# A scan kernel's order of work: a fourth product buffer, new due times, an ordered operand, and one more chunk before the loop's end

## The chip, the cores and the metric

The kernel runs on one core of one Trainium2 chip. A core has five engines that run side by side and meet only at semaphores: TensorE (PE in the profile; PEld is its weight load), VectorE (DVE), ScalarE (ACT), GpSimd (POOL) and SyncE (SP, which here only issues transfers). The metric is the device time of one execution, in microseconds: 31468.83 us is the median of three runs before the change (31461.65 to 31485.9). A profiled execution also gives a time for every instruction.

## The reference, cut to what matters

The input is a batch of 8 images of 128 channels and 64 x 64 points. A deformable 3 x 3 convolution is added to it. Its result is read as 8 sequences of 4096 tokens, and a selective scan runs over them; a mixture of experts follows.

```python
x = x + _L0_conv_ref(_gn(x), ...)              # deformable 3x3, four corners per tap
t = _to_tokens(x)                              # 8 x 4096 tokens of 128
xs, z = jnp.split(_ln_t(t) @ W_in, 2, axis=-1)
delta, Bv, Cv = xs @ W_delta, xs @ W_B, xs @ W_C
deltaA = jnp.exp(jnp.einsum('bld,dn->bldn', delta, A))
def step(state, inp):                          # state: 8 x 256 x 256
    dA_i, dB_i, x_i, C_i = inp
    state = dA_i * state + dB_i * x_i[:, None, :]
    return state, jnp.einsum('bdn,bn->bd', state, C_i)
t = t + (y * silu(z)) @ W_out                  # y: the steps' outputs
t = t + top-2 mixture of 8 experts of _ln_t(t)
```

The scan's state has 8 x 256 x 256 numbers, and each of the 4096 steps multiplies all of them by a decay, adds an outer product, and contracts them with a vector.

## The kernel before, in words

After a preparation (`prepare`, `images`: group norm, offsets, a table of cells in DRAM), a loop of 8 iterations covers 512 steps each. 16 steps are a block (`BL`), 2 steps a chunk (`CH`). On chip the state's 256 indices lie on 128 partitions in two halves, so that 8 images x 2 halves make 16 units of 256 columns. `SETS` deals them into five groups: groups 0 and 1 of four units and group 2 of three units live in SBUF (`ht`), group 3 of four units and group 4 of one unit live in PSUM (`ud`, `us`).

One step does this:

- `pair`: each group's state is multiplied by its decay `et` into a product buffer, by GpSimd for groups 0 to 2 and by VectorE for groups 3 and 4 (line 1310). Groups 0 and 1 share the pool `mt`, of three four-unit buffers; group 2 uses `m3`, group 3 `md`, group 4 `mh`, of two each.
- `units`: TensorE makes the outer products in three lots, into the single PSUM tile `up` for the groups in SBUF, and added in place onto `ud` and `us` for the others. VectorE adds product and `up` into `ht` (line 1325); ScalarE copies the products of groups 3 and 4 back to PSUM (line 1330), before the lot that adds to them.
- `contract`: TensorE contracts the products with `zc` into `yp`, groups 0 and 3 first, then 1, 2 and 4. A product buffer returns to its pool when its sum or copy and its contraction are both done.

For a later chunk, `decays` makes the exponents on TensorE in 19 groups, through three PSUM banks, and `grow` takes their exponentials on ScalarE into one of two `et` buffers (line 1224); it waits for all products of the chunk two before, which used the same buffer. `load_rows`, `load_terms` and `copy_c` bring the chunk's operands (`rt`, `uu`, `zc`), the first two through transfers on SP's queue.

Beside it, once a block: `conv_load` and `conv_gather` (nine indirect transfers that GpSimd issues in its own queue, line 724, into `g` buffers), `conv_scale` (VectorE, three taps at a time: 12 operations, after which three `g` buffers come free, into `w` buffers), `conv_mix` (transposes, the convolution's sum, a norm), `project` (the projections; its first matmuls after `xst` compute the rows, with a strided view of `xst` as one operand), `stores`, and `behind` (the gate, the output projection, the routing, the experts, the store).

The order on every engine is written out by a planner, `Schedule.run`, when the program is built. Each of these generators is a thread that yields operations with a modelled duration and a due time, in steps. The planner keeps a modelled clock for each engine, takes the engine that could start earliest, and among its operations that could start within a short wait (`"wait"` of `DUE`) picks the one due first. The chip then runs this order as it stands: every engine's queue is in order, and a late operation holds up all that is queued behind it. Windows such as `project` spread their due times evenly over a span of steps. At the loop's end the planner starts afresh, from the state that `before` lists: what is ready at the seam.

Of the kernel before, what the change touches and what calls it, by code (L numbers as in the profile page):

```python
# [15 lines left out]
P = 128  # L16
# [9 lines left out]
NH = 2  # L26
# [25 lines left out]
QP = 3  # L52
REC = 5 * TAPS
# [13 lines left out]
def dve_ns(n, scaled=0):  # L67
# [4 lines left out]
    "gather": -0.04,  # L72
    "add": 0.23,
    "state": -0.33,
    "back": 1.16,
    "exp": (0.77, 1.65),
    "decay": (-0.1, 1.61),
    "unit": 0.33,
    "contract": 1.65,
    "project": (6.72, 11.35),  # L80
    "behind": (0.16, 13.12),
    "conv_mix": (1.0, 18.4),
    "conv_scale": (-0.99, 14.0),
    "same": 0.1,
    "wait": (200, 100, 100, 50),
# [8 lines left out]
class Due:  # L94


    def __init__(self, at, gap=0.0):
        self.at, self.gap = at, gap


class Op:


    def __init__(self, eng, ns, fn, lat=None, mode=FULL, need=None, free=(),
                 sets=(), chain=True, then=None, lock=None, due=None):
# [5 lines left out]
        self.chain, self.then, self.lock, self.due = chain, then, lock, due  # L111


class Thread:
    def __init__(self, gen):
        self.gen, self.t, self.cur = gen, 0.0, None
        self.due, self.gap = 0.0, 0.0


class Schedule:  # L120


    def __init__(self, pools, events=()):
# [5 lines left out]
        self.threads = []  # L129

# [5 lines left out]
    def step(self, th, value):  # L136
        try:
            th.cur = th.gen.send(value)
            while isinstance(th.cur, Due):
                th.due, th.gap = th.cur.at, th.cur.gap  # L140
                th.cur = th.gen.send(None)
# [7 lines left out]
    def run(self):  # L149
        while self.threads:  # L150
# [12 lines left out]
            ready = []  # L163
            for th in self.threads:
# [4 lines left out]
                if o.need is not None:  # L169
                    if not self.pools[o.need]:  # L170
                        continue
                    at = max(at, min(x[0] for x in self.pools[o.need]))
# [6 lines left out]
                ready.append((at, due, th))  # L179
# [25 lines left out]
            if o.due is None:  # L205
                th.due += th.gap
# [15 lines left out]
def kernel(  # L222
# [344 lines left out]
    mt = several(3, [P, 4 * DIN], FP, "mt")  # L567
    m3 = several(2, [P, 3 * DIN], FP, "m3")
    md = several(2, [P, 4 * DIN], FP, "md")
    mh = several(2, [P, DIN], FP, "mh")  # L570
# [12 lines left out]
    gt4 = several(5, [P, 4 * P], FP, "g")  # L583
    wt = several(6, [P, P], FP, "w")
# [4 lines left out]
    xst = fix.tile([P, 2, P], FP, name="xst")  # L589
    dpt = fix.tile([P, 3, DIN], BF, name="dpt")  # L590
# [3 lines left out]
    yt = fix.tile([P, DIN], FP, name="yt")  # L594
# [6 lines left out]
    se = fix.tile([P, P], FP, name="se")  # L601
    ot = fix.tile([P, P], FP, name="ot")
    nst = {w: fix.tile([P, 12], FP, name=f"n{w}") for w in "tm"}

    ud = psf.tile([P, 4 * DIN], FP, name="ud")
    up = psf.tile([P, 4 * DIN], FP, name="up")
    yp2 = psf.tile([P, 2, DIN], FP, name="yp")
    yp, us = yp2[:, 0, :], yp2[:, 1, :]
    state = ht + [ud, us]
    banks = [psf.tile([P, 512], FP, name=f"bank{k}") for k in range(3)]  # L610
# [898 lines left out]
```

## Time and profile before

| | us |
|---|---|
| median of 3 runs | 31468.83 |
| lowest and highest | 31461.65, 31485.9 |
| profiled execution | 31237.92 |
| its span, first to last instruction | 31236.1 |
| first product of the scan starts | 589.9 |
| last product of the scan ends | 31203.7 |

The profiled execution's mean granted TensorE clock is 0.975 of full speed. The page's first part gives each engine's busy time and its share of the span. The groups that follow give a line, an engine, the tiles written and read, the count, the busy time, the mean duration in ns, and the idle time of the engine just ahead of them with the instruction that ended it. A list of waits sums that idle time by who ended it: in total, how often, and the longest. A wait for several semaphores is put down to the one that came last.

### The profile page before, as it was taken

What the parts mean: (1) busy time and instruction counts of PE and PEld (TensorE: products, weight loads), DVE (VectorE), ACT (ScalarE), POOL (GpSimd) and SP (SyncE); (2) the same over time, 40 slices, a digit from 0 to 9 for tenths busy, and PEclk for the clock granted to TensorE, in tenths of its full rate; (3) what the DMA queues carried; (4) which work ended last, traced back from release to release, by engine and by line L of the source; (5) the groups of instructions that cost most, each with busy time, mean ns of one, the idle gap of its engine ahead of it and who ended that gap; (6) DMA issues with size and microseconds to landing.
All of it is one profiled execution on the core that took longest, in us unless ns stands there. A gap on an engine that the chain in (4) does not pass through costs nothing. (4 is left out here: it accounts for less than half of the span.)

```text
span 31236.1 us, 831602 instructions
## 1 busy us (share of the span) xinstructions
PE 28259.1 (90%) x303717; PEld 15288.6 (49%) x303717; DVE 26324.7 (84%) x47747; ACT 25431.0 (81%) x57825; POOL 28812.6 (92%) x14692
## 2 busy tenths in 40 slices
PE   6999989999899998999989999899998999989998
PEld 2544444544444444445444444444444444444544
DVE  5888888888888888888888888888888888888888
ACT  3888888888888887888888888888887888888888
POOL 3999999999999999999999999999999999999999
PEclk8999999999999999999999999999999999999999
DMA  5222222222222222222222222222222222222222
GB/s 128 60 57 60 58 57 57 60 58 59 56 60 58 59 60 56 59 58 60 57 58 57 60 57 60 55 61 59 58 60 56 58 58 60 57 58 58 60 57 56
DMA packets 4782745, 1873.06 MB, mean 60 GB/s; under 512 B 3445427, under 2 KB 4616504, under 8 KB 4777592
## 3 DMA queue, kind: packets, MB, share of 16 engines
q1 hardware_dynamic: 4578768, 1167.03, 18.8%
q0 software_dynamic: 191904, 625.53, 7.3%
q8 instruction: 2417, 39.60, 0.5%
q10 hardware_dynamic: 7944, 26.87, 0.3%
q14 instruction: 1712, 14.02, 0.2%
HBM read 1284.96 MB, written 532.52 MB: 58 GB/s over the span
## 5 line engine op out<-in xcount | busy, mean ns | idle before, releaser
L1224 ACT ACTIVATE et<-bank 128x448 f32<-128x448 f32 (+1 forms) x40980 | 19045.6, 527 | 3626.9 <-PE bank L687 3020.5
L1310 POOL TENSOR_TENSOR mt<-et,ht 128x1024 f32<-128x1024 f32 x8192 | 19282.7, 2370 | 1470.3 <-PE yp L687 873.7
L687 PE MATMUL bank<-rt,alhs 126*128 126x224 bf16 (+1 forms) x81960 | 12273.7, 254 | 1446.2 <-ACT et L1224 646.8
L1325 DVE TENSOR_TENSOR ht<-mt,up 128x1024 f32<-128x1024 f32 x8192 | 9967.2, 1217 | 2659.9 <-PE ud L687 1858.5
L687 PEld LDWEIGHTS <-alhs 126*128 126x128 bf16 x81960 | 6764.4, 98 | 7662.1 <-issue 6817.5
L687 PE MATMUL yp<-mt,zc 128*32 128x256 f32 x65536 | 8719.8, 388 | 152.1 <-POOL mt L1310 75.8
L1310 POOL TENSOR_TENSOR m<-et,ht 128x768 f32<-128x768 f32 x4096 | 7480.4, 1826 | 38.9 <-DVE ht L1325 11.3
L687 PE MATMUL up<-uu 32*128 32x256 bf16 x45056 | 4838.3, 275 | 598.6 <-DVE ht L1325 523.5
L1310 DVE TENSOR_TENSOR md<-et,ud 128x1024 f32<-128x1024 f32 x4096 | 4973.2, 1214 | 110.7 <-PEq L1442 43.3
L687 PE MATMUL yp<-m,zc 128*32 128x256 f32 x24576 | 4451.6, 391 | 156.1 <-POOL m L1310 147.9
L1325 DVE TENSOR_TENSOR ht<-m,up 128x768 f32<-128x768 f32 x4096 | 3892.5, 950 | 566.1 <-PE up L687 527.7
L687 PE MATMUL yp<-md,zc 128*32 128x256 f32 x32768 | 4359.7, 387 | 0.0
L1330 ACT COPY ud<-md 128x1024 f32<-128x1024 f32 x4096 | 4275.0, 1044 | 93.7 <-DVE md L1310 84.7
L687 PEld LDWEIGHTS yp<-mt,zc 128*32 128x32 f32 x65536 | 3273.9, 110 | 1622.0 <-issue 544.9
L687 PEld LDWEIGHTS <-uu 32*128 32x128 bf16 x65541 | 1613.7, 92 | 3121.3 <-issue 2882.9
L724 POOL DMA_INDIRECT g<-table,rec x2322 | 2265.1, 975 | 411.1 <-issue 244.3
L687 PE MATMUL yp<-mh,zc 128*32 128x256 f32 x8192 | 2483.8, 385 | 0.0
L1310 DVE TENSOR_TENSOR mh<-et,yp 128x256 f32<-128x256 f32 x4096 | 1704.6, 416 | 452.1 <-PE yp L687 429.2
L687 PEld LDWEIGHTS yp<-m,zc 128*32 128x32 f32 x24576 | 1587.8, 109 | 926.2 <-issue 422.9
L1330 ACT COPY yp<-mh 128x256 f32<-128x256 f32 x4096 | 1595.4, 389 | 355.8 <-PE yp L687 218.3
L757 DVE SCALAR_TENSOR_TENSOR bank<-g,rec,bank 128x128 f32<-128x128 f32 x4644 | 1640.7, 353 | 84.6
L687 PE MATMUL ud<-uu 32*128 32x256 bf16 x16388 | 1623.8, 276 | 0.1
(207 smaller groups left out, 22566.9 us busy)
## 6 DMA issues: line engine op xcount, KB each, us to landing
rt<-rz SPq DMA_DIRECT2D x14350, 22.5 KB
uu<-pr SPq DMA_DIRECT2D x8196, 36.0 KB
pr<-dpt SPq DMA_DIRECT2D x3084, 48.0 KB
pr<-bpt SPq DMA_DIRECT2D x3084, 48.0 KB
rz<-dst SPq DMA_DIRECT2D x6939, 21.0 KB
g<-table,rec POOLq DMA_INDIRECT x2322, 3.5
rec<-recs SPq DMA_DIRECT2D x2064, 2.8 KB
table<-xc SPq DMA_DIRECT2D x24, 858.0 KB
```

Source lines behind the costliest of these rows:

```text
L687: nc.tensor.matmul(out, lhs, rhs, start=start, stop=stop, **kw)
L724: nc.gpsimd.indirect_dma_start(out=g, out_offset=None, in_=table, in_offset=bass.IndirectOffsetOnAxis(ap=rec[b % 2].bitcast(I32)[:, j : j ...
L757: nc.vector.scalar_tensor_tensor(out, gq, s, acc, ALU.mult, ALU.add)
L1224: nc.scalar.activation(ec[:, :, :, P * f + d0 : P * f + d0 + n], ps[:, m * f * NH : m * (f + 1) * NH].rearrange("p (h d t) -> p h t d", h= ...
L1310: (nc.gpsimd if g < QP else nc.vector).tensor_tensor(like(g, m), part(g, c, lo), like(g, state[g]), ALU.mult)
L1325: lambda m=m: nc.vector.tensor_tensor(ht[g], m, up[:, :n], ALU.add),
L1330: ACT, act_ns(n, True), lambda m=m: nc.scalar.copy(state[g], m),
```

## The change

- `mt` gets a fourth buffer. To make room, `g` goes from five to four, `w` from six to five, `yt` becomes the same tile as `yy`, `se` the same as `tn2`, and `ot` the same as `tn2t`.
- Lots, contractions, state tiles and sums become general (`LOTS`, `CLOTS`, `PIECES`); with the values given, each step has the same instructions of the same size. The order of the matmuls within the second contraction and the second lot changes.
- The due times change: windows get inner points between which they run straight; each group has its own time for its sum, copy and lots; a product's turn goes by its width (0, 4/11, 8/11 of a step in place of thirds). The second contraction is due half a step earlier. The modelled cost of a product becomes 167 + 2.105 n ns in place of 25 + 2.237 n, and of a gather 1150 in place of 970.
- Windowed work due more than 14.37 steps after the latest product or gather planned is passed over as long as other work is ready.
- The rows' operand is copied by ScalarE into a second tile, `xsl`, in the order in which the matmuls read it.
- At the seam, and before the loop, two chunks instead of one have their decays taken and their operands loaded.

```diff
-    mt = several(3, [P, 4 * DIN], FP, "mt")
+MBUF = {"mt": (4, 4), "m3": (2, 3), "md": (2, 4), "mh": (2, 1)}
...
-    gt4 = several(5, [P, 4 * P], FP, "g")
-    wt = several(6, [P, P], FP, "w")
+    gt4 = several(NGB, [P, 4 * P], FP, "g")
+    wt = several(5, [P, P], FP, "w")
...
-    yt = fix.tile([P, DIN], FP, name="yt")
+    yt = yy
...
-    se = fix.tile([P, P], FP, name="se")
-    ot = fix.tile([P, P], FP, name="ot")
+    se, ot = tn2, tn2t
...
-    "gather": -0.04,
-    "add": 0.23,
-    "state": -0.33,
-    "back": 1.16,
-    "exp": (0.77, 1.65),
-    "decay": (-0.1, 1.61),
-    "unit": 0.33,
-    "contract": 1.65,
-    "project": (6.72, 11.35),
-    "behind": (0.16, 13.12),
-    "conv_mix": (1.0, 18.4),
-    "conv_scale": (-0.99, 14.0),
-    "same": 0.1,
-    "wait": (200, 100, 100, 50),
+    "gather": -4.86,
+    "add": (0.57, -0.4, 0.79),
+    "state": (-0.42, -0.27),
+    "back": (1.56, 1.06),
+    "exp": (0.77, 1.68, 0.51),
+    "decay": (-0.13, 1.19, 0.537),
+    "unit": (0.31, -0.0, 0.07),
+    "contract": (1.63, 1.14),
+    "project": (6.72, 11.35, 0.448, 0.486, 0.75),
+    "behind": (0.05, 13.12, 0.25, 0.521, 0.685),
+    "conv_mix": (1.0, 18.37, 0.318, 0.497, 0.75),
+    "conv_scale": (-0.99, 14.1, 0.293, 0.5, 0.759),
+    "same": 0,
+    "wait": (200, 100, 100, 0),
+    "lead": 14.37,
...
-                ready.append((at, due, th))
+                ahead = o.due is None and due > self.now + DUE["lead"]
+                (later if ahead else ready).append((at, due, th))
+            ready = ready or later
...
             yield Op(
                 ACT, act_ns(DIN),
                 lambda: nc.scalar.copy(xst, wk[:, :DIN].rearrange("p (a b) -> p a b", a=2)),
-                free=release(wk),
+            )
+            yield Op(
+                ACT, act_ns(DIN),
+                lambda: nc.scalar.copy(
+                    xsl, wk[:, :DIN].rearrange("p (a b l) -> p a l b", a=2, b=QI)
+                ), free=release(wk),
             )
...
-                    xlb[:, h], start=(h == 0), stop=(h == 1),
+                    xsl[:, h].rearrange("p l b -> p (l b)"), start=(h == 0), stop=(h == 1),
...
-            s.add(decays(range(1, NC + 1)))
-            s.add(grow(range(1, NC + 1)))
-            s.add(load_rows(range(2, NC + 2)))
-            s.add(load_terms(range(1, NC + 1)))
-            s.add(copy_c(range(1, NC + 1)))
+            s.add(decays(range(2, NC + 2)))
+            s.add(grow(range(2, NC + 2)))
+            s.add(load_rows(range(3, NC + 3)))
+            s.add(load_terms(range(2, NC + 2)))
+            s.add(copy_c(range(2, NC + 2)))
```

## The prediction

> **What bounds the kernel now.** First the page's busy shares, then GpSimd's groups with the idle time ahead of them, then the list of its waits.
>
> ```profile
> span 31236.1 us, 831602 instructions
> PE 28259.1 (90%) x303717; PEld 15288.6 (49%) x303717; DVE 26324.7 (84%) x47747; ACT 25431.0 (81%) x57825; POOL 28812.6 (92%) x14692
> ...
> L1310 POOL TENSOR_TENSOR mt<-et,ht 128x1024 f32<-128x1024 f32 x8192 | 19282.7, 2370 | 1470.3 <-PE yp L687 873.7
> L724 POOL DMA_INDIRECT g<-table,rec x2322 | 2265.1, 975 | 411.1 <-issue 244.3
> ```
>
> ```profile
> POOL mt L1310 <- PE yp L687: 873.7, 518, 4.2
> POOL mt L1310 <- DVE ht L1325: 231.8, 364, 2.2
> POOL mt L1310 <- POOLq L1442: 185.9, 7, 26.9
> POOL mt L1310 <- ACT et L1224: 146.0, 343, 26.0
> POOL g L724 <- DVE w L757: 71.6, 268, 9.0
> ```
>
> GpSimd carries the run, TensorE is close behind. From the starts of GpSimd's products: a step without gather or wait lasts 6.43 us, a gather adds 1.13, so a block of 16 steps with its 9 gathers could take 16 x 6.43 + 9 x 1.13 = 113.1 us. Over 240 blocks away from the seams it takes 118.7. Counting the idle time by the step's place in the block, the wait on "PE yp" sits at two places only: 1.1 us at step 8, and 2.4 us at step 11. There a product has no free mt buffer, because the third product back has not been contracted. The next view cuts two blocks into steps 8-9, 10-14 and 15-23.
>
> ```profile
> 13335.70:13350.24 14.54, 13.22 (x160) 6.92 (x161) 13.27 (x23) 12.08 (x27) 12.97 (x7) 1.00 0.31 42
> 13350.24:13388.86 38.62, 37.56 (x396) 21.28 (x396) 32.83 (x56) 32.90 (x75) 36.40 (x20) 1.00 0.38 76
> 13388.86:13453.72 64.86, 57.52 (x628) 30.22 (x626) 55.31 (x108) 54.06 (x124) 63.05 (x33) 0.97 0.20 53
> ```
>
> ```profile
> 13570.83:13585.38 14.55, 13.23 (x160) 6.92 (x161) 13.29 (x23) 12.08 (x27) 12.97 (x7) 1.00 0.28 41
> 13585.38:13626.84 41.46, 40.43 (x396) 23.50 (x396) 32.79 (x56) 32.93 (x75) 36.35 (x19) 0.92 0.35 71
> ```
>
> The columns are length, then PE, PEld, DVE, ACT and POOL busy, then the granted clock. In steps 10-14 TensorE is full (37.56 of 38.62 us), in steps 15-23 it has 7.3 us to spare. The second block differs by its clock, and its stretch is 2.84 us longer. Here are its GpSimd rows, steps 10 and 11:
>
> ```profile
> 13587.71 2.37 POOL L1310 TENSOR_TENSOR mt<-et,ht 128x1024 f32<-128x1024 f32 x1
> 13590.03 1.82 POOL L1310 TENSOR_TENSOR m<-et,ht 128x768 f32<-128x768 f32 x1
> 13595.97 4.71 POOL L1310 TENSOR_TENSOR mt<-et,ht 128x1024 f32<-128x1024 f32 x2 [4.12 <-PE yp L687]
> ```
>
> The wait is 4.12 us where the undisturbed block has 1.24. The granted clock is 0.50 from 13587.3 for 6.8 us. In all, 669 us of half clock fall into step 10, 6.83 us at a time: 98 dips. Blocks with one last 119.9 us, blocks without any 117.0. The sum below holds nothing for dips beyond what sits inside the mt wait. TensorE's longest gap just ahead of this dip is 0.68 us. [...]
>
> **The change, part by part.** *A fourth mt buffer.* The product at step 11 then needs the fourth product back, whose contraction ended at 13347.3 in the first block, 9.4 us before GpSimd was ready for it (13356.7). Bounds: nothing, or all 873.7 us (3.4 a block). What is late next is TensorE. Without moving its work, steps 10-14 can shrink from 38.62 to its 37.56 us, and steps 8-9 from 14.54 to its 13.22: 2.4 us. A dip's lag can now run into the slack of steps 15-23. I take 2.5 us a block, the TensorE bound being the nearest row: 256 x 2.5 = 640 us gained. [...]
>
> *Rows' operand copied in order.* One more ACT copy a block (L903's mean 377 ns; 257 of them, 97 us of ACT), ahead of the exponentials in ACT's queue; the first row matmul waits for it. The matmuls lose their strided operand:
>
> ```profile
> L687 PE MATMUL bank<-xst,wdelta_sb x2056: 378/393/579, 555.1 to 31146.1; 128*128 128x128 f32 x187
> L687 PE MATMUL bank<-xst,wc_sb x2056: 275/275/389, 584.3 to 31198.5; 128*128 128x128 f32 x187
> ```
>
> The strided form has a median of 393 ns, the ordered one of the same size 275: 8 x 118 = 0.94 us a block off TensorE, at steps 7-8. ACT's 0.38 us hides in its 19.7 us of idle time a block; without that cover it is +97 us. TensorE's 0.94 us is worth at most 240 us. Steps 8-9 are already counted down to TensorE's bound, so I add 0.
>
> *g buffers five to four, w six to five.* A gather waits at the head of GpSimd's queue with all products behind it. Group by group, three g buffers come free together after 12 scale operations on DVE. In the steady order the gathers for taps 4, 7 and 8 would each meet such a release; now only tap 8 does, at step 3, and it makes the 71.6 us row. Two more of that kind would be +143 us. The planner can put a gather behind a product instead, which costs nothing, so I take half: +70. The ends are 0 and +1250, the latter reckoned in the slower rival. The w buffer's lender is TensorE's transposes, three steps away: 0.
>
> *Due times, inner points, unit split, lead.* The instructions of units, adds and contractions stay the same in number and size. Units 1 and 2 are due 0.3 and 0.2 steps earlier, the second contraction half a step, the late decays 0.45 step. Product waits on "DVE ht" (231.8 us) come from late units on TensorE; a quarter of them goes: -60, ends -232 and +232 (the same again, at other steps). The lead limit holds back only windowed work that is over 14.37 steps ahead of the products; everything with such a window waits on products of nearer steps: 0. The new product and gather costs (2322.5, 1783.6 and 1150 ns) fit the 6.43 and 1.13 above; they change order alone.
>
> *One more chunk ready at the seam.* The whole program gains one chunk: 20 exponentials and 40 decay matmuls, about 10.5 us of ACT at 527 ns, ahead of the first product (which now waits 26 us on "ACT et"). In each of eight tails another chunk moves in front of the loop's end, with 7 rt and 4 uu transfers on SP's queue and one zc copy. The tail is bound by a serial chain of the routing: GpSimd idles 26.55 us, ACT nearly all of it, SP has one issue there. The exponentials can delay ACT's few links by up to one each, 1.5 us a seam: +12. In return the block after a seam, now 123.5 to 126.5 us against 118.7, loses some of its excess; no product there waits on et, since nine gathers are bunched in its steps 1 and 5, so I take 3 us x 7 = -21. Net 0, ends -40 and +110.
>
> *Shared tiles* (yt on yy, se on tn2, ot on tn2t): each new writer comes after the old reader in one dependent chain; the next block's write of tn2t follows the store by 16 steps: 0.
>
> **Sum.** -640 + 70 - 60 = -630 on the profiled execution's own 31237.92 us (span 31236.1): 30,608. The median of the runs shown, 31468.83, is 1.0074 times the profiled execution; kept as a ratio, the forecast is 30,608 x 1.0074 = 30,834, say 30,830.
>
> **The rivals.** *The wait moves to et.* At step 12 a product already waits 0.3 us for exponentials, which wait 3020 us in all for "PE bank"; their chunk can only begin when step 9's products end. If TensorE's order there is as tight as now, 2.4 us of step 11 turn up at step 12, and only step 8's 1.05 us stay won: 270 us, 30,968 x 1.0074 = 31,197. For it: PE 97% full in steps 10-14. Against: decays are due earlier, and mixing later.
>
> *More is won.* The dips go too. They cost 98 x 2.9 = 284 us at step 10, of which the 2.5 us a block holds about half; 74 at steps 3 and 4 cost 1.3 us each, 96 us. With those, the rest of ht (172) and of mt (234), about -1200: 30,038 x 1.0074 = 30,260. For it: 113.1 us is the floor, 5.6 below today. Against: TensorE's 108.3 us a block would then be 95% of the 114.0 left.
>
> *Slower: the gathers hold up the products.* DVE's scale operations start 391 ns apart, the planner counts 255: after 12 of them a release is 1.6 us later than planned. Three stalls of 1.6 us a block are 256 x 4.9 = 1250 us: 30,608 + 1180 = 31,788, x 1.0074 = 32,020. It decides from 2.5 us a block on. Against: the one gather now in that place waits 0.16 us.
>
> *Nothing is won.* The planner's new order trades waits one for another, within 0.2% (about what a measurement of this kernel can tell from no change).
>
> **How the numbers follow.** Forecast 0.48; more 0.17; moved to et 0.15; nothing 0.06; slower 0.14. Faster is 0.80, same 0.06, slower 0.14. The forecast's own range is 30,450 to 31,100. The given range goes from 30,150, near the sum of the best ends, to 31,420, just above the bound of "same", and leaves out the slower case and the far end of the larger gain.
>
> **What would show it.** Right: the wait of mt on "PE yp" under 200 us, blocks near 116 us, row matmuls at 275 ns, "g <- DVE w" at 70 to 220 us, the seam still 26 to 29 us. Wrong: an "ACT et" wait near 600 us, a "g" wait near 1000, more half-clock stretches than now, or idle time of TensorE in steps 10-14 while GpSimd waits.

## The result, and the profile after

The changed kernel takes 31863.85 us (median of four runs, 31820.26 to 31920.63), where the kernel before, on the same chip, took 31470.04: a ratio of 1.0129, with a 95% interval of 1.0117 to 1.0141. It is slower, by 1.3%. The forecast was 30,830 us, its range 30,150 to 31,420.

The kernel before itself took 31,204 to 31,250 us in four sets of runs and 31,449 to 31,470 us in three others, and its profiled execution (31237.92 us) is like the first four while that of after (31875.81 us, span 31874.1) belongs to one of the three, so every ratio below is against the kernel before within the same set, and a block time compared across traces can be off by up to 0.8%.

From the page of after, its span and busy shares and five of its groups (busy time, mean ns, idle time ahead of the group and what ended most of it):

```profile
span 31874.1 us, 827006 instructions
PE 27903.7 (88%) x303757; PEld 15061.6 (47%) x303757; DVE 26102.5 (82%) x47747; ACT 25693.7 (81%) x58103; POOL 28786.1 (90%) x14692
...
L1256 ACT ACTIVATE et<-bank 128x448 f32<-128x448 f32 (+1 forms) x41000 | 18955.0, 524 | 3518.6 <-PE bank L715 2639.3
L1389 POOL TENSOR_TENSOR mt<-et,ht 128x1024 f32<-128x1024 f32 x8192 | 19232.7, 2369 | 1537.4 <-ACT et L1256 985.1
L715 PE MATMUL bank<-rt,alhs 126*128 126x224 bf16 (+1 forms) x82000 | 12074.9, 255 | 1882.2 <-ACT et L1256 977.9
...
L715 PE MATMUL up<-uu 32*128 32x256 bf16 x45056 | 4843.6, 274 | 1118.5 <-DVE ht L1410 983.6
...
L752 POOL DMA_INDIRECT g<-table,rec x2322 | 2256.0, 972 | 991.7 <-DVE w L785 463.9
```

The work is the same to within 1%: GpSimd is busy 28786 us against 28813. What grew is idle time, and it has new owners. The list of GpSimd's waits after the change (total, times, longest):

```profile
POOL mt L1389 <- ACT et L1256: 985.1, 751, 25.9
POOL g L752 <- DVE w L785: 463.9, 284, 9.5
POOL mt L1389 <- DVE ht L1410: 279.5, 154, 5.8
POOL mt L1389 <- POOLq L1551: 235.2, 7, 33.9
...
POOL g L752 <- PE ud L715: 164.0, 69, 2.9
```

The wait on "PE yp", 873.7 us before, is gone from the list; there is not one case of it in the steady blocks. In its place the wait on "ACT et" rose from 146 to 985 us, and gathers now wait 464 us for VectorE's scale operations (72 before) and 164 us more for "PE ud". On TensorE the wait on "DMA rt<-rz" is new, the one on "DVE ht" has nearly doubled and the one on "ACT et" has grown by two fifths. Its list of waits after, then the same two from before:

```profile
PE up L715 <- DVE ht L1410: 983.6, 2555, 2.1
PE bank L715 <- ACT et L1256: 982.5, 2982, 1.3
PE bank L715 <- DMA rt<-rz: 414.2, 199, 3.7
```

```profile
PE bank L687 <- ACT et L1224: 691.4, 2338, 0.7
PE up L687 <- DVE ht L1325: 523.5, 1504, 2.0
```

By the starts of GpSimd's products, over 240 blocks away from the seams (a block's time moves by about 0.1 us with the step at which blocks are cut). A half-clock stretch is a stretch of time in which the granted clock of TensorE is 0.50:

| us | before | after |
|---|---|---|
| block of 16 steps | 118.77 | 120.94 |
| GpSimd's wait on "PE yp", a block | 3.48 | 0 |
| on "ACT et" | 0.43 | 3.78 (steps 8, 10, 12) |
| gathers, on "DVE w" and "PE ud" | 0.16 | 2.4 (2.2 of it at step 15) |
| on "DVE ht" | 0.89 | 1.05 |
| first product starts | 589.9 | 610.1 |
| step with a seam in it | 33.0 | 40.1 |
| last product's end to the span's end | 32.4 | 40.5 |
| half-clock stretches of TensorE in 240 blocks | 185 | 245 |

Blocks: 256 x 2.17 = 556 us; seams: 20 + 7 x 7 + 8 = 77 us; together 633 of the 638 us between the two profiled executions. (The pair of medians differs by 394. Of the other 244, 232 are there because the traced execution of before was that much faster than the median it is compared with, and 12 because that of after was slower.)

The last line of the table became the main matter of this study. Four stretches of before, around step 10 of the disturbed block that the prediction showed, cut where the clock changes (columns: length, then PE, PEld, DVE, ACT and POOL busy, then the granted clock):

```profile
13580.47:13583.89 3.42, 3.02 (x35) 1.57 (x35) 3.21 (x9) 2.77 (x8) 3.42 (x3) 1.00 0.45 53
13583.89:13587.30 3.41, 2.36 (x23) 1.41 (x22) 3.36 (x6) 2.32 (x7) 2.90 (x2) 1.00 0.48 46
13587.30:13590.71 3.41, 3.41 (x17) 2.84 (x15) 2.05 (x3) 2.34 (x5) 3.41 (x3) 0.51 0.33 61
13590.71:13594.13 3.42, 3.42 (x23) 2.51 (x23) 0.73 (x1) 1.29 (x3) 1.14 (x1) 0.50 0.34 67
```

TensorE is busy 2.36 of 3.41 us (0.69), and then its clock is halved for two stretches of that same length. In after, the same at step 14, where TensorE waits for "DMA rt<-rz":

```profile
13168.54:13171.95 3.41, 3.21 (x41) 1.62 (x34) 3.41 (x4) 1.89 (x5) 3.40 (x3) 1.00 0.38 89
13171.95:13175.36 3.41, 0.37 (x3) 0.10 (x3) 1.98 (x5) 0.71 (x3) 3.25 (x3) 1.00 0.27 62
13175.36:13178.78 3.42, 3.12 (x22) 1.15 (x22) 0.42 (x1) 1.53 (x4) 2.69 (x2) 0.50 0.54 143
```

### The profile page after: what moved, and what is told of

Same layout as the page of the kernel before. It is cut to its first block, busy times and chain, and to the rows that moved or that the text cites. A ratio compares the mean times of both kernels' runs of the same rounds, so it can differ in the third digit from the quotient of the medians.

```text
span 31874.1 us, 827006 instructions
## 1 busy us (share of the span) xinstructions
PE 27903.7 (88%) x303757; PEld 15061.6 (47%) x303757; DVE 26102.5 (82%) x47747; ACT 25693.7 (81%) x58103; POOL 28786.1 (90%) x14692
## 5 line engine op out<-in xcount | busy, mean ns | idle before, releaser
L715 PE MATMUL bank<-rt,alhs 126*128 126x224 bf16 (+1 forms) x82000 | 12074.9, 255 | 1882.2 <-ACT et L1256 977.9
L715 PEld LDWEIGHTS <-alhs 126*128 126x128 bf16 x82000 | 6650.7, 98 | 7887.8 <-issue 7089.3
L715 PE MATMUL yp<-mt,zc 128*32 128x256 f32 x65536 | 8876.5, 392 | 273.7 <-DVE mh L1389 158.3
L715 PE MATMUL yp<-md,zc 128*32 128x256 f32 x32768 | 4442.7, 393 | 0.0
L715 PEld LDWEIGHTS <-uu 32*128 32x128 bf16 x65541 | 1794.8, 92 | 3728.2 <-issue 3356.0
L715 PEld LDWEIGHTS yp<-md,zc 128*32 128x32 f32 x32768 | 1572.6, 110 | 0.0
```

What stands on the lines that cost most here:

```text
L715: nc.tensor.matmul(out, lhs, rhs, start=start, stop=stop, **kw)
```

## The experiments

Eighteen kernels. Some keep the order of every queue as it was (e5, e6, e7, e9, e11 to e15, e17 and e18, against their parent) and change something under it; others go through the planner again, which then writes a new order, and this turned out to matter as much as what was changed.

### Parts of the change, one at a time

**e4_before_seam**: the kernel before with the seam of after.

```diff
-            s.add(decays(range(1, NC + 1)))
+            s.add(decays(range(2, NC + 2)))
...                                # and grow, load_rows, load_terms, copy_c
```

> The kernel before with two chunks ready at the seam alone. The prediction on record said net 0 (ends -40 and +110). By the changed kernel's trace: the first product starts 20 us later, each of seven seams is 7 us longer, the end 8 us: +77 us, 31,547; the blocks between as before.

Measured: 1.0024 (1.0014 to 1.0033), +73 us. First product at 600 us, the seam step 38.7 us, the end 38.0. So the extra chunk lengthens the start, each seam and the end, and nothing comes back behind it in sum: the block after one of the seven seams takes 124.4 to 125.8 us (123.5 to 126.5 before) and the one behind that 123.1 to 124.8 (116.7 to 117.8 before; the two traces are of different sets).

**e1_straight_project**: the kernel after, with the window of the projections without inner points.

```diff
-    "project": (6.72, 11.35, 0.448, 0.486, 0.75),
+    "project": (6.72, 11.35),
```

> The changed kernel with the projection's window straight again (no inner points), all else as changed. Theory A (late rows): the inner points put the row matmuls at step 11 of the block instead of 7.5 to 8, so the rows reach DRAM late, the next block's first rt transfer lands late, TensorE stands 1.7 us at step 14 and its clock halves in about half of the blocks; then the rt wait and the half clock at step 14 go, and with them the 1.0 us of 'DVE ht' and most of the 0.7 us of 'PE ud' at step 15: 2 to 3 us a block, 500 to 750 us off the changed kernel, 31,100 to 31,350. Theory B (four g buffers alone hold up step 15): at most 150 us off. Theory C (planner's luck: any new order moves the time by about 1% either way): no particular wait goes.

Measured: 1.0106 (1.0090 to 1.0123). The inner points had moved the row matmuls from steps 7.5 to 8 to step 11, so their rows reach DRAM at steps 11.5 to 13.5 and the next block's first `rt` load comes late, at step 14. With the straight window the wait on "DMA rt<-rz" is gone and so are the half-clock stretches of step 14 (3 are left of some 120), as Theory A expected; but the block falls only to 120.5 us, and the gain of some 75 us is far from its 500 to 750. In the new order products wait on "ACT et" (3.0 us a block) and "DVE ht" (2.6) at other steps.

**e2_five_g**: the kernel after with five `g` buffers (room from `w`, four, and shared tiles), planned anew. **e7_new_order_g5**: the order of after as it stands, its gathers dealt over five tiles.

```diff
-    gt4 = several(NGB, [P, 4 * P], FP, "g")
-    wt = several(5, [P, P], FP, "w")
+    gt4 = several(5, [P, 4 * P], FP, "g")
+    wt = several(4, [P, P], FP, "w")
...                                # e7 only: the planner still counts NGB = 4
+                if o.need in self.real:
+                    item = next(self.real[o.need])      # the next of five in turn
```

> The changed kernel with five g buffers (room from w four, and from xs and the gate's transpose sharing tiles that are idle then). Theory B: the gather's waits at step 15, 'DVE w' 1.5 us and 'PE ud' 0.7 us a block (628 us in all), go, 500 to 600 us off: 31,250 to 31,350. Theory A: the stall of step 14 stays, the product behind the gather waits instead, 0 to 250 us off. Under both the 'ACT et' waits at steps 8, 10 and 12 (3.75 us a block) stay.

> The changed kernel's order kept instruction for instruction (the planner sees four g buffers), with five tiles behind it. Theory B: the gather's waits of 2.2 us a block at step 15 ('DVE w' and 'PE ud') go, and 400 to 600 us with them. Theory A and E: the time goes to the product behind the gather ('DVE ht' at step 15, or et at the next chunk): 0 to 200 us off.

Measured: e2 1.0109 (1.0092 to 1.0126), e7 1.0067 (1.0048 to 1.0086). GpSimd's waits in e7:

```profile
POOL mt L1394 <- ACT et L1261: 1038.4, 766, 28.3
POOL mt L1394 <- DVE ht L1415: 353.8, 330, 3.4
POOL g L757 <- issue: 256.7, 1432, 0.3
```

The gathers' waits on "DVE w" and "PE ud" fall from 2.4 us a block to under 0.1, and "ACT et" and "DVE ht" of the products rise by 0.5. Against after's 1.0129 the ratio is 0.62% lower, some 195 us, the end of what Theories A and E expected and half of Theory B: the largest single part of the loss that was found, but an uncertain one. After was measured in a set in which before takes 31,470 us, e7 in one in which it takes 31,217, and a ratio can shift by about 0.5% between two such sets (e17 below). Planned anew (e2, in a set like that of after), the same buffer gives 0.2%; the new order waits more on "DVE ht" (1.9 us a block).

**e3_before_mt4** and **e5_old_order_mt4**: the kernel before with a fourth `mt` buffer; e3 planned anew, e5 with the order of before and `mt` dealt over four tiles. To make room, `w` has four tiles in both and some small tiles are shared; in e5 the old order still counts six, so a `w` tile can be rewritten before it is transposed and some taps of the convolution come from another group, with the amount of work unchanged.

```diff
-    mt = several(3, [P, 4 * DIN], FP, "mt")
-    wt = several(6, [P, P], FP, "w")
+    mt = several(4, [P, 4 * DIN], FP, "mt")
+    wt = several(4, [P, P], FP, "w")
```

> The kernel before with a fourth mt buffer alone (room from w four and shared tiles; five g buffers, old due times, old seam). The prediction on record: the wait on 'PE yp' goes and 2.5 us a block stay won: 640 us off, 30,830. Theory D (what ends the product's wait next is et, since the next chunk's exponentials end just as GpSimd asks for them): 'PE yp' goes to under 100 us, 'ACT et' rises by 300 to 700 us, 0 to 350 us off, 31,120 to 31,470. Theory C: anything within 1%.

> The order of the kernel before, kept instruction for instruction (the planner still sees three mt buffers), while the tiles behind them rotate through four (w's six through four tiles; yt, se, ot and the gate's transpose on shared tiles). So the wait for a free mt buffer goes and nothing else moves. The prediction on record: 2.5 us a block won, 30,830. Theory E (the loop of decays on TensorE, three PSUM banks and exponentials on ScalarE sets the pace; the product that no longer waits for a buffer waits for et): 'PE yp' under 100 us, 'ACT et' and 'DVE ht' up by most of that, 0 to 350 us won, 31,110 to 31,460. Theory C (planner's luck made e3 slower): not slower than before here, since the order is the old one.

Measured: e3 1.0043 (1.0027 to 1.0060), e5 0.9993 (0.9983 to 1.0003). In e3 the order is new, and products wait 2.6 us a block on "ACT et" and 2.2 on "DVE dpt". e5 is the central result on the change. GpSimd's waits in e5:

```profile
POOL mt L1314 <- DVE ht L1329: 896.0, 1078, 3.2
POOL g L728 <- issue: 253.9, 1568, 0.3
...
POOL mt L1314 <- ACT et L1228: 192.2, 344, 26.0
```

Where the fourth buffer is added and nothing reordered, the 873.7 us on "PE yp" are gone, and "DVE ht" rises from 231.8 to 896.0 us. By step, 3.5 us a block of "PE yp" at steps 8 and 11 give way to 2.7 more of "DVE ht", at steps 9 to 11, and 0.2 more of "ACT et", at step 12. Blocks without a half-clock stretch last 116.96 us against 116.97 before. The buffer buys nothing that can be told from zero: the product that no longer lacks a buffer lacks its state. The two `w` tiles fewer are not the cause: VectorE has no wait over 0.15 us ahead of a write to `w`, neither before nor in e5.

### What holds the units up

A state is late when VectorE's addition to it is late. In e5, of 3.2 us a block that products wait for a state at steps 9 to 11, 1.8 stand behind an addition that itself waited for its unit lot on TensorE, and 1.4 behind one that VectorE began without a wait, right after other work. The chain of work that ended last, followed back, spends 72% of steps 10 and 11 in TensorE's matmuls, over the 30 late blocks that it covers. Here are its shares in one of them:

```profile
by line: PE bank L691 49.7%; PE yp L691 19.2%; PE up L691 10.5%; ACT et L1228 8.6%; DVE ht L1329 7.9%; DVE w L761 3.3%; issue 1.7%; PE ud L691 0.2%; DVEq L1329 0.0%
```

Theory F of the expectations says that TensorE is simply full in steps 9 to 13.

**e6_half_exponentials**: e5 with half the columns of each exponential left out.

```diff
-                            ec[:, :, :, P * f + d0 : P * f + d0 + n],
+                            ec[:, :, :, P * f + d0 : P * f + d0 + n // 2],
```

> As e5, and each exponential covers half of its columns, at the same place in the same order (half of the decays stay at a constant 1, so half of the exponentials are left out). ScalarE loses some 4 us of work a chunk. Theory E: the et wait goes, blocks of 114 to 116 us, 700 to 1100 us under the kernel before. Theory F (TensorE, full in steps 10-14, is the pace): its matmuls are all still there, blocks stay at 118 or more, at most 250 us won over e5.

Measured: 0.9872 (0.9853 to 0.9892). ScalarE's busy time falls from 98.9 to 75.9 us a block, the wait on "ACT et" to nothing, but 3.3 us a block still wait on "DVE ht" (3.6 in e5). The block takes 117.2 us, between what Theory E (114 to 116) and Theory F (118 or more) expected: ScalarE's work counts for 1.2 us a block, but it is not what the late states wait for.

**e9_half_decays**: e6, and the decay matmuls compute only the half that is still read.

```diff
-                                alhs[:KR, g + f, P * h : P * h + P], rv[:, :n, g + f, :],
+                                alhs[:KR, g + f, P * h : P * h + P],
+                                rv[:, : n // 2, g + f, :],
```

> As e6_half_exponentials, in the same order, and the decay matmuls now compute only the half of the columns that the halved exponentials still read (112 instead of 224 moving columns in each of 320 matmuls a block); the other half of the exponentials stays left out. It takes TensorE work away in every step and nothing else. Theory F (in steps 9 to 13 TensorE itself is full, so units are multiplied late, their additions on VectorE are late, and GpSimd waits on 'DVE ht'): the 3.3 us a block that e6 still waits on 'DVE ht' fall under 0.8, the block from 117.2 to 115 or less, the ratio to about 0.968 (0.960 to 0.975). Theory G (the lateness lies in the written order: a unit stands behind an instruction that waits for another engine): the wait on 'DVE ht' stays above 2.3 us a block and the ratio within 0.983 to 0.990.

Measured: 0.9954 (0.9936 to 0.9972). Both theories missed. With less work for TensorE the kernel got slower than e6, by 0.8%. The core's span and mean granted clock, then that of e6, then three stretches around a step 10 of e9:

```profile
core 0: 31109.1 us, clock 0.928
```

```profile
core 0: 30835.4 us, clock 0.973
```

```profile
12933.61:12937.02 3.41, 1.70 (x26) 1.07 (x19) 3.25 (x8) 1.43 (x7) 3.15 (x3) 1.00 0.49 45
12937.02:12940.43 3.41, 3.24 (x17) 2.18 (x16) 3.30 (x4) 2.87 (x7) 3.41 (x2) 0.50 0.42 61
12940.43:12943.85 3.42, 3.42 (x24) 2.90 (x23) 0.00 (x0) 0.74 (x3) 2.38 (x2) 0.50 0.33 73
```

The mean clock is 0.928 where e6 had 0.973, and there are 739 half-clock stretches in 240 blocks in place of 186. TensorE, given less to do, was idle for half of 12933.61 to 12937.02 and got half the clock for what came next, which is the crowded part. So the test of Theory F is spoiled by something stronger. One reading in its favour stays, beside the chain above: in e6, blocks without a half-clock stretch last 115.49 us and wait 1.65 us on "DVE ht", where those with one at step 9 last 119.52 and wait 5.7; states are late when TensorE is slow. That TensorE's full queue is the whole cause is not shown.

**e15_new_order_half**: e7 (order of after) with half of each exponential left out, as in e6.

> The order of after with g over five tiles, as e7_new_order_g5 (1.0067, 4.0 us a block waited on 'ACT et'), and half of each exponential's columns left out, as in e6. If 'ACT et' is the loss that is left: that wait goes to under 0.5 us, the block from 119.5 to about 115.5 (half-clock stretches may take a part back), the ratio to 0.973 (0.965 to 0.985). If TensorE is as late there and et only stands in front: the wait turns into 'DVE ht' and the ratio stays above 0.995.

Measured: 0.9953 (0.9937 to 0.9968), at the edge of what the second reading expected (above 0.995), but the wait does not turn into "DVE ht" (1.4 us a block, as in e7). "ACT et" falls from 3.99 to 2.70 us a block and no further. At step 12 it does not move at all (1.72 to 1.82 us). The chunk that step 12 needs takes 15.59 us from its first exponential to its last in e7, of which 10.28 are exponentials and 1.56 waits on "PE bank"; with half the columns it takes 15.65, with 7.04 of exponentials, 3.31 on "PE bank" and 1.39 on "DVE md". Halving the exponentials does not shorten it; the waits on the decays on TensorE and on VectorE's products fill the time instead, and the name "ACT et" in the list of waits only names the last link.

### The order itself

**e8_nudged_order**: the kernel before with one due time changed by a hundredth of a step.

```diff
-    "unit": 0.33,
+    "unit": 0.34,
```

> The kernel before with one due time moved by a hundredth of a step (units 0.33 to 0.34), nothing else. It measures how much a change of the order without a meaning moves the time. Theory C: 100 to 400 us either way (0.3 to 1.3%), more likely slower, since 0.33 was the value kept. If orders that near are alike: within 60 us.

Measured: 0.9956 (0.9940 to 0.9973). The new order has 59 half-clock stretches instead of 185. Blocks without one are slower than before's (117.83 against 116.97 us); it wins by the clock alone.

**e16_after_old_due**: the kernel after with the due times, gaps and modelled costs of before (the products' turns by width stay).

```diff
-    "unit": (0.31, -0.0, 0.07),
-    "contract": (1.63, 1.14),
+    "unit": (0.33, 0.3, 0.27),
+    "contract": (1.65, 1.65),
...                                # and so for every entry of DUE; "lead": 1e9
```

> The kernel after with the due times, gaps and planner's costs of before: four mt, four g and five w buffers, the ordered copy and the new seam stay. From e3 (1.0043 for four mt buffers in a new order) and e4 (0.0024 for the seam), with up to 0.006 for four g buffers: 1.007 to 1.013 if the buffers and the seam make the loss, whatever the due times; under 1.004 if the new due times make it.

Measured: 1.0373 (1.0356 to 1.0390). With the new buffers, the old due times are 2.4% worse than the new ones (the sets of e16 and after differ, so to some 0.5%): products wait 1506 us on "DVE ht", 3.0 us a block at step 1 and 2.4 at step 12. The new due times belong to the new buffers.

**e10_three_undone**: after with the straight window of e1, five `g` tiles as in e7, and the old seam.

> The kernel after with three parts undone together: the projection's window without inner points, gathers over five g buffers (w over four), and the loop's seam as before. If the three add up as measured alone (0.23% for the rows' place, 0.62% for the gathers, 0.24% for the seam, from 1.0129): 1.002 (1.000 to 1.004), block 118.9 us, first product near 590 us, seam step near 33 us, and what is left is the wait on 'ACT et', 3 to 4 us a block. If they hide behind one another (a wait that goes gives way to 'ACT et' in the same steps): 1.006 or more, block above 119.8.

Measured: 1.0133 (1.0117 to 1.0148). The three gains did not add, they vanished. The seam is back (first product 583 us, seam step 32.1) and no gather waits; but the planner wrote another order, with 268 half-clock stretches (124 at step 2, 86 at step 4), 3.4 us a block on "ACT et" and 3.2 on "DVE ht", 120.6 us a block. Its blocks without a half-clock stretch last 119.03. So an account that adds up parts measured in different orders does not hold for this kernel, mine in e10's expectation included.

### The rows' copy, and the clock

**e11_rows_copy_alone**: before with the ordered copy, issued with the first copy so that no queue changes order; its room comes from sharing `yt`, `se` and `ot` as in after. **e12_nudged_rows_copy**: the same on e8's order.

```diff
-                lambda: nc.scalar.copy(xst, ...),
+                lambda: [nc.scalar.copy(xst, ...), nc.scalar.copy(xsl, ...)],
...
-                    xlb[:, h], start=(h == 0), stop=(h == 1),
+                    xsl[:, h].rearrange("p l b -> p (l b)"), start=(h == 0), stop=(h == 1),
```

> The kernel before with the rows' operand copied in order and nothing else; the second copy is issued right behind the first, so that the order of every queue stays. Row matmuls 393 to 275 ns, 0.94 us a block off TensorE at steps 7 and 8; ScalarE gets 0.38 us a block. The prediction's step said 0. If TensorE's work ahead of steps 9 to 13 counts (Theory F), up to 0.94 us a block: 0.998 (0.9925 to 0.999). If ScalarE's copy stands in the way of the exponentials: 1.003.

> The nudged order of e8_nudged_order (units due 0.34 instead of 0.33) and the rows' copy of e11_rows_copy_alone. If the two add: 0.9956 times what e11 gives, about 0.993 (0.989 to 0.996). If the nudge's gain was luck of that chip, within 0.3% of 1.

Measured: e11 0.9940 (0.9926 to 0.9953), e12 0.9931 (0.9917 to 0.9945). Of the 0.7 us a block in e11's trace, 0.26 are in the blocks without a half-clock stretch (116.71 against 116.97 us); the rest goes with there being 141 such stretches instead of 185.

**The clock, from the records of the traces.** In each trace every half-clock stretch begins on one grid of 3413 ns (to within 35 ns). Cutting the trace of before along that grid, and asking after each full-clock interval whether the next is at half:

| TensorE's busy share in an interval | intervals | next one at half clock |
|---|---|---|
| under 0.60 | 57 | 55 |
| 0.60 to 0.68 | 187 | 119 |
| 0.68 to 0.70 | 88 | 35 |
| 0.70 to 0.72 | 69 | 3 |
| 0.72 and more | 8177 | 0 |

The busy share alone does not sort the intervals. In the trace of after, 25 of 8135 intervals with a share of 0.72 or more were followed by half clock, in e10 62 of 8167; and in e3 only 11 of 216 between 0.60 and 0.68. The kind of work went with it too: over the 20 traces, intervals between 0.60 and 0.68 were followed by half clock in 883 of 1460 cases where they held next to no contraction of a product (under 3% of the interval), and in 376 of 2732 where they did; between 0.68 and 0.72 in 476 of 1317 and 105 of 2877. Why is open.

If a low share is cause and not company, TensorE must get faster by being given more to do.

**e13_filled_gaps** and **e14_rows_copy_filled**: eight more decay matmuls a block, ahead of three unit lots at which TensorE waits for VectorE; on before, and on e11.

```diff
+    FILL = {(9, 1): 2, (3, 1): 1, (1, 2): 1}
+    def again(j, p):
+        for k in range(FILL.get((j % BL, p), 0) if live else 0):
+            list(live.values())[-1]()         # a pair of decay matmuls once more
     def lot(c, lo, groups):
+        again(CH * c + lo, {0: 0, 1: 1, 2: 2}[groups[0]])
```

> The kernel before with more work for TensorE and nothing less: ahead of three unit lots of a block that wait for VectorE (gaps of 662, 442 and 296 ns on TensorE), the latest pair of decay matmuls is issued once more (twice ahead of the first), eight matmuls of 224 columns a block; it writes the same values to the same bank again. Theory K (the clock is halved for at least 3413 ns after a stretch of 3413 ns in which TensorE was busy for less than some 0.7): the 98 half-clock stretches of step 10 fall under 15, those of steps 3 and 4 by half, and with 2.9 and 1.3 us each the ratio is 0.991 (0.987 to 0.995). Rival (the clock answers to load, or the gaps are without effect): eight matmuls more a block in a full TensorE cost up to 1.3 us a block: 1.000 to 1.011.

> e11_rows_copy_alone and e13_filled_gaps in one. e11's blocks without a half-clock stretch last 116.7 us against 118.1 over all. Theory K: 0.994 of e11 less up to 1.2 us of 118.1: 0.985 (0.981 to 0.990). Rival: 0.994 or more.

Measured: e13 0.9885 (0.9869 to 0.9902), e14 0.9860 (0.9844 to 0.9876): both inside what Theory K expects. The mean granted clock and the decay matmuls of e13, with what they waited for:

```profile
core 0: 30825.3 us, clock 0.991
```

```profile
L687 PE MATMUL bank<-rt,alhs 126*128 126x224 bf16 x75796 | 12016.2, 260 | 1314.8 <-ACT et L1226 479.3 <-DVE gate L1118 81.6 <-ACT zc L1164 35.2
```

The clock was 0.975 before. Half-clock stretches fall from 185 to 19 (e13) and from 141 to 10 (e14), the 97 of step 10 to none. Blocks without one are as before (116.98 us), so the whole gain of e13 is the clock. In the kernels that ran, the repeated pair was that of the next group of columns, not the same one as the expectation says, so some exponentials get other values; the added work is the eight matmuls (x75796 of 224 columns against x73764).

**e17_rows_copy_zero_fill** and **e18_rows_copy_zero_to_yp**: fills that multiply by zeros, on e11.

```diff
# e17, in `live`, for the pair above
+                            ps[:, :m], zw[:KR], alhs[:KR, 0, :m], start=False, ...
# e18
+    FILL = {(9, 1): 4, (3, 1): 2}
+    def nothing(j, p):
+        for k in range(FILL.get((j % BL, p), 0)):
+            mm(yp, zw[:KR], alhs[:KR, 0, :], start=False, skip_group_check=True)
```

> As e14_rows_copy_filled, but the matmuls in the gaps multiply by a tile of zeros and add to a bank that a decay has filled, so that they change no value: two of 224 columns ahead of the lots with gaps of 442 and 296 ns, four ahead of that with 662 ns. If the clock answers to TensorE being occupied, whatever the numbers: 0.986 (0.984 to 0.989), under 30 half-clock stretches in 240 blocks. If zeros do not count as work: the stretches stay near e11's 141 and the ratio near 0.994 to 0.998.

Measured: 0.9988 (0.9979 to 0.9997). It tells little: two matmuls a block were issued, at the 442 ns gap alone; at the other lots no bank was waiting any more, the 662 ns gap stayed, and so did the half-clock stretches (169). They also changed a part of that bank's values, so that some exponentials are others. e17 also did worse than e11 in blocks without a half-clock stretch (117.98 us against 116.71), with new waits at steps 0, 1 and 14. These belong to the set of runs: products of e4, from another set in which before takes over 31,450 us, wait at the same steps (0.28, 0.42 and 0.37 us a block), while those of before, e11, e13, e14 and e18, traced in sets in which it takes 31,204 to 31,250, do not. So a ratio to before can shift by some 0.5% from one such set to another (0.9940 against 0.9988 for the same order, with the two fill matmuls between them). What differs between the sets stays open.

> The kernel before with the rows' copy of e11 in the same order, and matmuls of a tile of zeros (126x128 weights, 256 columns bf16) that add nothing to yp: four ahead of the unit lot with the gap of 662 ns, two ahead of the one with 296 ns, six a block. If the clock answers to TensorE being occupied, whatever the numbers: under 40 half-clock stretches in 240 blocks (e11: 141), a block near 116.9 us, ratio 0.986 (0.983 to 0.990). If multiplying by zeros does not count: the stretches stay near 141 and the ratio is 0.994 to 0.999.

Measured: 0.9854 (0.9837 to 0.9870), 30773.71 us against 31231.91. This beats both kernels, the kernel after by 2.7% if its ratio is carried over. Its span and busy shares, clock, longest waits of GpSimd, the added matmuls, and two stretches around a step 10, the gap and what follows it:

```profile
span 30768.7 us, 834716 instructions
PE 27840.2 (90%) x305253; PEld 15043.0 (49%) x305253; DVE 26296.2 (85%) x47748; ACT 25428.1 (83%) x58082; POOL 28804.4 (94%) x14692
```

```profile
core 0: 30768.7 us, clock 0.991
```

```profile
POOL mt L1321 <- PE yp L689: 519.4, 528, 1.6
POOL g L726 <- issue: 251.1, 1555, 0.3
```

```profile
L689 PE MATMUL yp<-alhs,zw x1536: 269/270/284, 616.9 to 30690.8; 126*128 126x256 bf16 x192
```

```profile
13259.32:13262.73 3.41, 2.77 (x26) 1.57 (x24) 3.32 (x7) 2.32 (x8) 2.88 (x2) 1.00 0.50 49
13262.73:13266.15 3.42, 3.37 (x30) 2.80 (x33) 2.40 (x4) 3.02 (x7) 3.42 (x3) 1.00 0.31 42
```

The interval with the gap now has 2.77 us of work (0.81) instead of 2.36 and the clock stays at 1.00 behind it; 15 half-clock stretches are left in 240 blocks, and the longest wait of `mt` on "PE yp" is 1.6 us where it was 4.2. The block takes 116.88 us. (118.77 - 116.88) x 256 = 484 us is the gain by the traces; 458 us is that of the medians. Against e11, which has the copy without the fill, the ratio is 0.9% lower.

## Why the prediction was wrong

- **The fourth `mt` buffer: "2.5 us a block, the TensorE bound being the nearest row".** This step failed. The wait on "PE yp" did go, to nothing, as "what would show it" asked. But e5 gives 0.9993 with the order kept: where 640 us were to be won, some 20 were, and that lies within the interval of nothing. Most of the wait came back as "DVE ht", at steps 9 to 11 (2.7 of 3.5 us a block). This is 640 of the some 1,020 us between the forecast change (-630) and the measured one (+394). I took the busy sum of TensorE over steps 10 to 14 (37.56 of 38.62 us) as the time to which they could shrink. A unit lot has its place in a queue that is 97% full, behind decays and contractions, and the additions have theirs on VectorE; shrinking the stretch would have needed the lots and the additions earlier, and the freed product met a state that was not ready. That the state is what was late is shown (e5); why it was late is shown in part only. The rival "nothing is won" had this outcome, but named another mechanism.
- **Rows' copy: 0.** The duration was right (275 ns, below). The value was wrong: alone it is worth 0.60% (188 us) in the set of e11, close to the bound of 240 us that I had put aside. I had bounded it by TensorE's work only and did not see that taking 0.94 us out of the queue also changes how many half-clock stretches there are (141 in place of 185). And in after the rows did not stay at steps 7 and 8; I had not seen that the inner points move them to step 11, with 414 us of "DMA rt<-rz" on TensorE. The row of these matmuls in after:

```profile
L715 PE MATMUL bank<-xsl,wdelta_sb x2056: 274/275/583, 574.1 to 31797.6; 128*128 128x128 f32 x187
```

- **Four `g` buffers: +70, ends 0 and +1250.** Some +195 us (e7 against after, uncertain by about 0.5%, 160 us), inside the ends. The mechanism of the slower rival was there, at one place (step 15, 2.2 us a block) rather than three.
- **Due times: -60, ends -232 and +232.** This term was mis-sized too. Among the new buffers the due times move the time by 2.4% (e16), some 750 us and over three times the bound, though in the gaining direction; no run has them with the buffers of before. A bound taken from one wait in the old order says nothing of a new order.
- **Seam: 0, ends -40 and +110.** Measured +73 to +77 us. The 21 us that I let come back did not.
- **Shared tiles: 0.** Nothing speaks against it (e5 and e11 have them), though they were not tried alone.
- **The rival "the wait moves to et"** named the wait that the list of after shows largest (985 us) and gave 31,197, still faster. It let only one wait move and nothing else get worse, and in e5, where the order is kept, the wait moved to "DVE ht".
- **The clock.** I saw the 98 half-clock stretches at step 10 and that they cost 284 us, found that no gap before them was longer than 0.68 us, and then left them alone as something given ("the sum below holds nothing for dips"). Their number goes with the order, 185 in one and 59 in another, and most of them are worth 1.2% (e13). "Less TensorE work is a gain or nothing" stands behind two of my steps, and e9 shows it to be false here (0.9954 against e6's 0.9872).

What stays open: how much of after's 1.29% is "ACT et" and "DVE ht" in its order and how much its 245 half-clock stretches. The seam (0.24%) is shown within one set, the gathers (0.62%) only across two. Blocks of after without a half-clock stretch last 119 to 120 us against 116.97 before, but the two traces come from executions of different speed.

## What to carry to other kernels

When a wait for a free buffer goes, ask whether the next thing that the instruction needs, here its state, would have been ready at that time; test it with the order kept, by dealing the same instructions over one more tile. Where a planner writes the order, every edit is also a new draw of the order, worth 0.4% here for a due time moved by a hundredth of a step (e8); an edit is measured with the order held, and an order by several small nudges. And look at the granted clock before counting TensorE's idle time as free: a short gap at a wrong place was dearer here than six matmuls that fill it (0.9940 in e11, 0.9854 with them in e18).

## What the hardware showed that I had not expected

- Half clock came by a fixed length of time, and after short gaps. In each trace of this case half-clock stretches began only on one grid of 3413 ns (to within 35 ns); in the trace of before none came after an interval with 0.72 or more of TensorE busy (0 of 8177), after one under 0.60 nearly always (55 of 57), and a stretch lasted one interval or more (6.83 us, two of them, at step 10). Ahead of the stretches at step 10 the two longest gaps within the interval were 0.67 and 0.20 us in the mean. Matmuls put into the gaps took most stretches away (185 to 19 in e13, 141 to 15 in e18). In other orders the counts part less cleanly (after: 25 of 8135 at 0.72 or more), and at the same share intervals without contractions were followed by half clock more often (at 0.60 to 0.68, 883 of 1460 against 376 of 2732 over the 20 traces). Beyond these counts nothing was shown of why the clock is halved.
- With matmuls of an all-zero weight tile in the gaps the half-clock stretches fell too (e18: six a block, 270 ns each, from 141 in e11 to 15; the moving operand, `alhs`, was not zero).
- Less TensorE work made the program slower: e9 against e6, 0.9954 against 0.9872, at a mean clock of 0.928 against 0.973.
- The same kernel differed by 0.8% between sets of runs (31,204 to 31,470 us), more than most parts of this change.
